# Layer 1's quantised FFN as a step pipeline in written order on four engines

## The chip, the cores and the metric

One NeuronCore of a Trainium2 chip runs the whole program. The metric is the device time of one execution in microseconds (us). The engines are called as the profile calls them: PE (TensorE, matrix products and transposes), DVE (VectorE), ACT (ScalarE), POOL (GpSimd) and SP (SyncE, which issues most transfers).

## The reference

A four-layer gated network on `x` of 128 x 64 x 128 floats. Each layer adds a gated cross-attention and a gated FFN of the layer-normed `x`; the four attentions and the four FFNs differ from each other. Only layer 1's FFN matters here. Its two linear maps quantise activations row by row to whole numbers of 8 bits and the weights to -1, 0 and 1:

```python
def rmsnorm(x):
    return x * jax.lax.rsqrt(jnp.mean(x * x, axis=-1, keepdims=True) + EPS)
def act_quant(x):
    scale = 127.0 / jnp.clip(jnp.max(jnp.abs(x), axis=-1, keepdims=True), 1e-05)
    q = jnp.clip(jnp.round(x * scale), -128.0, 127.0) / scale
    return x + jax.lax.stop_gradient(q - x)
def bitlinear(x, w, b):
    xq = act_quant(rmsnorm(x))
    wq = weight_quant(w)
    return jnp.einsum('bsd,fd->bsf', xq, wq) + b
...
    h = bitlinear(x, w1, b1)            # 128 -> 512
    h = jax.nn.gelu(h, approximate=False)
    return bitlinear(h, w2, b2)         # 512 -> 128
...
x = x + jnp.tanh(g_ffn[1]) * _L1_ffn_ref(_layernorm(x, axis=-1), ...)
```

## The kernel before

The 8192 tokens are 64 tiles of 128 rows (`NT` = 64). `x` stays in on-chip memory in float32 (`x_sb`) through all layers. The program is written in Python as a sequence of engine instructions; a scheduler then chooses each engine's order of instructions from its own estimates, within the data dependences, and sets the semaphores. Where a piece of code stands in a `tc.manual_schedule(engines=...)` block, the engines named follow the order in which the instructions are written. The scheduler may also pull instructions of a later stage into an earlier one.

Layer 1's FFN is `bit_ffn`. It runs over the 64 tiles in groups of `G` = 8:

- `bit_normal(g)` (L1472, POOL): eight `tensor_scalar` of 128x128, `xn_g` = the layer norm of the group's tiles, from the columns `nm` and `rstd`.
- `bit_sizes(g)` (L1484 to L1494, DVE): the rows' absolute maxima, one reduction of 128x1024, and a chain of small operations on 128x8 (`steps`, L1362 to L1369), which gives the factors `up` and `dn` and, in three bfloat16 pieces, the factor `inv` of the bias.
- `bit_whole(g, h)` (L1502, L1505, DVE): rounds four tiles of `xn_g` to whole numbers. It is called for the two halves.
- `first(g)` (L1535 to L1545): eight PE transposes of 128x128 (`pxq`), two copies by ACT (`xqT`), two transposes of the `inv` pieces (`pinv`) and a copy by ACT (`invT`).
- `second(k)`: two matmuls of 512 columns into `ph` (L1554 and L1556, PE), GELU into `h` (L1560, ACT), the square with its sum (`sq`, L1563, ACT), and the row maxima of `h` (`am`, L1564, DVE).
- `third`, once a group, when all eight tiles have their sum and maximum: 17 small DVE operations on 128x8, each of which needs the one before it (L1572, `quick_root` at L216 to L222, `steps`); its last result is `up` (L1369).
- `fourth(i)`: two `tensor_scalar` of 128x512 that round `h` in place (L1578, L1579; on POOL, and on DVE for every second tile of the last group, called `own`), four PE transposes (`phq`, L1582), ACT's copy to `hqT` (L1584), four matmuls into `py` (L1587, PE), and `residual`: `x_sb` += `dn` x `py` (L295, DVE) and the statistics `st` of the new `x` (L198, DVE). Every four tiles POOL first adds the gated bias `b2g` to `x_sb` (L1608).

The loop has steps i = 0 to `NT` + `LAG`, with `LAG` = `G` + 3 = 11: step i calls `second` for tile i and `fourth` for tile i - 11. `third` is called at the end of a group's last step. The next group's `bit_normal`, `bit_sizes` and the halves of `bit_whole` are called in steps k = 1, 3, 5 and 6 of a group. Four further pieces of DVE work are spread into the loop: `norms_of` with its root (L225 to L262; small operations on 128x32) for the second half of the tiles at i = 10, the root mean squares of that half (`rms_square`, L242) at i = 18, and the norms that the next attention needs at i = 56 and 64. None of this is in a `manual_schedule` block, so that the calls give the data dependences, and the scheduler the order.

The accumulators in PSUM are `pt`, `ph`, `pt4` and `py`, two buffers each. `hqT` has two buffers, `h` has `LAG` + 4 = 15, `xn_g` two.

Ahead of `bit_ffn` stands attention 1 (`head_attention(1, ...)`). Its lines in the prediction are the reciprocal L1004 and the transposes L1022 at the end of an attention step, which turn the heads' outputs; the next step's work on PE is queued behind them. Group 0's `bit_normal` is called within attention 1 by a plan; other early parts of the FFN get there by the scheduler's choice.

Of the kernel before, what the change touches and what calls it, by code (L numbers as in the profile page):

```python
# [14 lines left out]
ALU = mybir.AluOpType  # L15
AX = mybir.AxisListType
PE = mybir.EngineType.PE
SP = mybir.EngineType.SP
ACT = mybir.EngineType.Activation
DVE = mybir.EngineType.DVE  # L20
POOL = mybir.EngineType.Pool
# [5 lines left out]
P = 128  # L27
D = 128
# [13 lines left out]
class Net:  # L42
# [1315 lines left out]
    def steps(self, am, r, size, up, down, inverse=None):  # L1358


        nc = self.nc
        nc.vector.tensor_mul(am, am, r)  # L1362
        nc.vector.tensor_scalar_max(am, am, 1e-5)
        nc.vector.tensor_scalar(down, am, size, None, ALU.mult)
        nc.vector.reciprocal(am, am)
        if inverse is not None:
            nc.vector.tensor_scalar(inverse[0], am, inverse[1], None, ALU.mult)
        nc.vector.tensor_mul(am, am, r)
        nc.vector.tensor_scalar_mul(up, am, 127.0)  # L1369
# [141 lines left out]
    def bit_ffn(self):  # L1511

        nc, tc, NT = self.nc, self.tc, self.NT
        G = 8
        NG = NT // G


        LAG = G + 3  # L1520
        t1, t2, less, size2, r1 = self.t1, self.t2, self.less, self.size2, self.r1
        self.next_stats()
        with ExitStack() as st:
            work = st.enter_context(tc.tile_pool(name="bf", bufs=2))
            psum = st.enter_context(tc.tile_pool(name="bf_ps", bufs=2, space=PSUM))

            def first(g):

                b = self.bit_xn.pop(g)
                xn, dn = b["xn"], b["dn"]  # L1530
                xT = []
                for h in range(0, G, 4):
                    pt = psum.tile([P, 4, P], F32, tag="pt", name="pxq")
                    for k in range(4):
                        nc.tensor.transpose(pt[:, k, :], xn[:, h + k, :], self.ident)  # L1535
                    t = work.tile([P, 4, P], BF16, tag="xqT", name="xqT", bufs=4)
                    nc.scalar.activation(t, pt, AF.Identity, bias=less)
                    xT.append(t)
                pi = psum.tile([P, 2, P], BF16, tag="pt", name="pinv")
                for h in range(2):  # L1540
                    nc.tensor.transpose(
                        pi[:, h, :], self.inv[g % 2][:, h].rearrange("p k x -> p (k x)"), self.identb
                    )
                inv = work.tile([P, 2, P], BF16, tag="invT", name="invT")
                nc.scalar.copy(inv, pi)  # L1545
                hid = {}
                ss = work.tile([P, G], F32, tag="ss", name="ss")
                am = work.tile([P, G], F32, tag="am2", name="am2")
                return xT, inv, dn, hid, ss, am

            def second(k, xT, inv, dn, hid, ss, am):

                ph = psum.tile([P, FF], F32, tag="ph", name="ph")
                nc.tensor.matmul(ph, lhsT=xT[k // 4][:, k % 4, :], rhs=t1, start=True, stop=False)  # L1554
                rows = slice(32 * (k % 4), 32 * (k % 4) + 32)
                nc.tensor.matmul(  # L1556
                    ph, lhsT=inv[rows, k // 4, :], rhs=self.b1p[rows, :], start=False, stop=True
                )
                hid[k] = work.tile([P, FF], F32, tag="h", name="h", bufs=LAG + 4)
                gelu = nc.scalar.activation(hid[k], ph, AF.Gelu, scale=dn[:, k : k + 1])  # L1560
                self.last_own = gelu.ins.name
                sq = work.tile([P, FF], F32, tag="sq", name="sq")
                nc.scalar.activation(sq, hid[k], AF.Square, accum_out=ss[:, k : k + 1])  # L1563
                nc.vector.tensor_reduce(  # L1564
                    am[:, k : k + 1], hid[k], AX.X, ALU.max, apply_absolute_value=True
                )

            def third(ss, am):
                up = work.tile([P, G], F32, tag="up2", name="up2")
                dn = work.tile([P, G], F32, tag="dn2", name="dn2")  # L1570
                r = work.tile([P, G], F32, tag="r2", name="r2")
                nc.vector.tensor_scalar(ss, ss, 1.0 / FF, RMS_EPS, ALU.mult, ALU.add)  # L1572
                self.quick_root(r, ss, work, G)
                self.steps(am, r, size2, up, dn)
                return up, dn

            def fourth(i, k, h, up, dn, eng):
                eng.tensor_scalar(h, h, up[:, k : k + 1], MAGIC, ALU.mult, ALU.add)  # L1578
                eng.tensor_scalar(h, h, MAGIC + 127.0, MAGIC - 128.0, ALU.min, ALU.max)  # L1579
                pt = psum.tile([P, 4, P], F32, tag="pt4", name="phq")  # L1580
                for c in range(4):
                    nc.tensor.transpose(pt[:, c, :], h[:, c * P : (c + 1) * P], self.ident)  # L1582
                hT = work.tile([P, 4, P], BF16, tag="hqT", name="hqT")
                nc.scalar.activation(hT, pt, AF.Identity, bias=less)  # L1584
                py = psum.tile([P, D], F32, tag="py", name="py")
                for c in range(4):
                    nc.tensor.matmul(  # L1587
                        py, lhsT=hT[:, c, :], rhs=t2[:, c * D : (c + 1) * D],
                        start=(c == 0), stop=(c == 3),
                    )  # L1590
                self.residual(i, py, dn[:, k : k + 1])

            self.bit_sizes(0)
            self.bit_whole(0, 0)
            self.bit_whole(0, 4)
            groups, scales = {}, {}
            for i in range(NT + LAG):
                g, k = i // G, i % G
                if i < NT:
                    if k == 0:  # L1600
                        groups[g] = first(g)
                    second(k, *groups[g])
                if i >= LAG:
                    j = i - LAG
                    if j % 4 == 0:

                        x = self.x[:, j : j + 4, :]
                        nc.gpsimd.tensor_tensor(  # L1608
                            x, x, self.b2g.unsqueeze(1).to_broadcast([P, 4, D]), ALU.add
                        )  # L1610

                    own = j >= NT - G and j % 2
                    up, dn = scales[j // G]
                    fourth(j, j % G, groups[j // G][3][j % G], up, dn, nc.vector if own else nc.gpsimd)
                if i < NT and k == G - 1:
                    scales[g] = third(*groups[g][4:])
                if g + 1 < NG:
                    if k == 1:
                        self.bit_normal(g + 1)
                    elif k == 3:  # L1620
                        self.bit_sizes(g + 1)
                    elif k in (5, 6):
                        self.bit_whole(g + 1, 4 * k - 20)
                half = NT // 2
                if i == 10:
                    v = self.norms_of(half, half, self.st6_for, nc.vector)
                    self.norms_root(half, half, v)
                if i == 18:
                    ms = self.rms_square(half, half, v, nc.vector)
                    self.quick_root(r1[:, half:], ms, self.stat, half)  # L1630

                if i == NT - 8:
                    self.norm_columns()
                    v = self.norms_of(0, half, self.st6, nc.vector)
                    self.norms_root(0, half, v)
                if i == NT:
                    v = self.norms_of(half, NT // 4, self.st6, nc.vector)
                    self.norms_root(half, NT // 4, v)
        self.bit_stack.close()


# [564 lines left out]
```

## Time and profile before

| | |
|---|---|
| time, median of 3 runs (lowest to highest) | 2637.76 us (2636.06 to 2638.65) |
| the profiled execution: its time | 2637.47 us |
| its span, first to last instruction | 2635.7 us |
| mean granted TensorE clock | 0.911 of full speed |
| layer 1's FFN, first `pxq` transpose to the last `st` | about 1286 to 1475.5 us of the span |

The profile is of one execution. Its busy shares are means over stages that differ much; a stage is read by giving the views a window of time. In a line of the groups stand the line of the code, the engine, the operation, what it writes and reads, how many there were, the busy time in us and the mean of one in ns, and then the engine's idle time just before these instructions with what ended most of it. In a line of the timeline stand the start and the duration in us.

### The profile page before, as it was taken

The numbers are of one execution on the slowest core, as the hardware profiler recorded it, in microseconds if no ns is written. First come the engines' busy times: TensorE is split into PE (matmuls) and PEld (weight loads), VectorE is DVE, ScalarE is ACT, GpSimd is POOL, SyncE is SP. The second block draws the span as 40 slices with busy tenths as digits, with TensorE's granted clock in tenths as the row PEclk, the third lists the DMA queues.
The fourth block names the chain that finished last, engine by engine and source line by source line (L and its number), as shares of the span: only waits on it lengthen the run. The fifth ranks groups of instructions, "written<-read, shape, count | busy, mean of one in ns | idle before, by whom it ended". The sixth has DMA issues, their size and how long they took to land.

```text
span 2635.7 us, 75540 instructions
## 1 busy us (share of the span) xinstructions
PE 2200.8 (83%) x31658; PEld 1694.6 (64%) x31658; DVE 1548.2 (59%) x4442; ACT 1354.3 (51%) x2697; POOL 1053.9 (40%) x1309
## 2 busy tenths in 40 slices
PE   5999999999984978969767799998499867777597
PEld 4777777777773756757434576766499745555465
DVE  5544455454553337666677657676577588888432
ACT  3445454444442424546577455554377557777242
POOL 2122242233234552131266313634566662444444
PEclk9999999999996988989777899998699879888699
DMA  9997000000002141000000001111233541111121
GB/s 235 259 233 154 14 20 24 10 24 20 15 17 74 54 130 38 19 14 15 5 1 1 21 20 35 47 30 37 62 94 91 154 120 34 38 36 36 50 63 44
DMA packets 215364, 157.42 MB, mean 60 GB/s; under 512 B 27236, under 2 KB 191983, under 8 KB 215024
## 3 DMA queue, kind: packets, MB, share of 16 engines
q1 hardware_dynamic: 193744, 117.22, 18.4%
q0 software_dynamic: 16640, 32.22, 3.6%
q8 instruction: 250, 4.10, 0.7%
q10 hardware_dynamic: 4640, 3.15, 0.5%
q14 instruction: 90, 0.74, 0.1%
HBM read 68.62 MB, written 86.31 MB: 59 GB/s over the span
## 4 chain that ended last, share of the span: by engine, by line
PE 57%; DVE 18%; ACT 9%; POOL 5%; DMA 5%; issue 4%; SPq 0%; DVEq 0%; POOLq 0%; ACTq 0%
PE pqk L423 9%; PE ph L2009 5%; PE py L519 4%; PE pv L445 4%; PE po L505 3%; PE pav L982 3%; PE py L2030 2%; PE sb L924 2%; PE ph L1276 2%; PE sc L461 2%; PE pt L489 2%; PE pye L1295 2%; ACT low L965 2%; PE sb L931 2%; ACT low L963 2%
## 5 line engine op out<-in xcount | busy, mean ns | idle before, releaser
L478 POOL TENSOR_TENSOR a<-a,sm 128x1024 f32<-128x1024 f32 x64 | 121.7, 1901 | 449.3 <-DVE sm L477 228.6
L936 ACT ACTIVATE aT<-sb 128x512 f32<-128x512 f32 x256 | 132.1, 603 | 170.4 <-PE sb L931 170.4
L897 DVE TENSOR_REDUCE mpad<-sa 128x8 f32<-128x512 f32 x256 | 159.0, 684 | 85.6 <-PE sa L892 85.5
L524 DVE TENSOR_TENSOR x_sb<-x_sb,py 128x128 f32<-128x128 f32 x64 | 18.4, 288 | 284.2 <-PE py L519 284.2
L492 ACT COPY aT<-pt 128x512 f32<-128x512 f32 x128 | 68.8, 589 | 207.4 <-PE pt L489 207.4
L2040 POOL DMA_INDIRECT outs<-ye,to x136 | 133.7, 983 | 78.1 <-DVE ye L2036 54.4
L1875 POOL DMA_INDIRECT slots<-x_sb,fc_r x128 | 124.8, 975 | 96.8 <-DVE fc_r L1223 46.8
L786 POOL TENSOR_SCALAR xn<-x_sb,gn_nm,gn_r 128x128 f32<-128x128 f32 x128 | 57.7, 463 | 255.9 <-PE pxn L801 171.7
L982 PE MATMUL pav<-aT,vb 128*32 128x64 f32 x6144 | 127.0, 235 | 29.9 <-DVE aT L968 20.0
L423 PE MATMUL pqk<-xnT,L_Wq 128*128 128x256 f32 x512 | 120.9, 390 | 21.4 <-ACT xnT L415 21.4
L982 PEld LDWEIGHTS pav<-aT,vb 128*32 128x32 f32 x6144 | 106.0, 119 | 48.3 <-DVE aT L968 24.1
L2009 PE MATMUL ph<-xT,gw 128*128 128x128 f32 x1088 | 133.8, 277 | 0.0
L445 PE MATMUL pv<-L_Wv,ctxT 128*64 128x512 f32 x480 | 129.5, 618 | 0.0
L519 PEld LDWEIGHTS py<-L_wog,oT 128*128 128x128 f32 x1024 | 124.2, 192 | 7.4 <-DVE oT L510 4.2
L1295 PEld LDWEIGHTS pye<-L_w,hT 128*128 128x128 f32 x1024 | 119.1, 192 | 14.3 <-issue 11.2
L2009 PEld LDWEIGHTS ph<-xT,gw 128*128 128x128 f32 x1088 | 128.1, 194 | 0.2 <-issue 0.2
L519 PE MATMUL py<-L_wog,oT 128*128 128x128 f32 x1024 | 125.0, 275 | 3.8 <-DVE oT L510 3.8
L423 PEld LDWEIGHTS pqk<-xnT,L_Wq 128*128 128x128 f32 x512 | 96.0, 192 | 41.1 <-ACT xnT L415 29.1
L1295 PE MATMUL pye<-L_w,hT 128*128 128x128 f32 x1024 | 119.2, 275 | 0.0
L505 PEld LDWEIGHTS po<-aT,v 64*64 64x64 f32 x4096 | 77.7, 136 | 63.3 <-ACT aT L492 51.5
L1276 PE MATMUL ph<-xeT,L_w 128*128 128x512 f32 x256 | 117.4, 602 | 0.0
L963 ACT ACTIVATE low<-low 128x512 f32<-128x512 f32 x128 | 80.3, 628 | 70.6 <-DVE low L956 70.4
(363 smaller groups left out, 5932.3 us busy)
## 6 DMA issues: line engine op xcount, KB each, us to landing
slots<-zero SPq DMA_DIRECT2D x80, 528.0 KB
ctxT<-in_ctxT_dram SPq DMA_DIRECT2D x63, 256.0 KB
y<-outs SPq DMA_DIRECT2D x24, 512.0 KB
xe<-slots SPq DMA_DIRECT2D x136, 66.0 KB
xe<-slots SPq DMA_DIRECT2D x32, 264.0 KB
L_w<-in_L_ffn_W_dram SPq DMA_DIRECT2D x32, 256.0 KB
outs<-fxn SPq DMA_DIRECT2D x16, 256.0 KB
out_dram<-x_sb SPq DMA_DIRECT2D x16, 256.0 KB
```

The source lines that it names most:

```text
L423: nc.tensor.matmul(ps[:, cc, :], lhsT=wt[:, (c + cc) * P : (c + cc + 1) * P], rhs=rhs, start=True, stop=True,)
L445: nc.tensor.matmul(ps[h * S : (h + 1) * S], lhsT=tok, rhs=wv[:, h], start=True, stop=True)
L505: nc.tensor.matmul(po[h][x * S : (x + 1) * S, s, tok], lhsT=v[rows, b, 2 * s + x, :], rhs=aT[rows, 2 * s + x, tok], start=True, stop=True,)
L519: nc.tensor.matmul(py, lhsT=oT[:, h, s, :], rhs=w["wog"][:, h, s, :], start=h == 0 and s == 0, stop=h == 1 and s == 3,)
L897: nc.vector.reduce_max(mpad[:, j, 0:8], sc[j].rearrange("p b c k -> p (b c) k"), axis=AX.X)
L936: exp = nc.scalar.activation(aT[:, j], sc[j], AF.Exp)
L963: ln = self.nc.scalar.activation(low, low, AF.Ln, bias=1.0, scale=-1.0)
L982: nc.tensor.matmul(pav[32 * j : 32 * j + 32, b, t, :], lhsT=vb[:, 4 * (b0 + b) + j, t, :], rhs=aT[:, j, b, t, :], start=True, stop=True,)
L1276: nc.tensor.matmul(ph, lhsT=w["w1"][:, e, c * P : (c + 1) * P], rhs=x, start=True, stop=True)
L1295: nc.tensor.matmul(py[:, t, :], lhsT=h[:, c, t * P : (t + 1) * P], rhs=w["w2"][:, e, c, :], start=(c == 0), stop=(c == 3),)
L2009: nc.tensor.matmul(ph[:, 2 * t + c, :], lhsT=gw[j][:, t, c * P : (c + 1) * P], rhs=xT[j // 4][:, j % 4, :], start=True, stop=True,)
L2040: put = nc.gpsimd.indirect_dma_start(out=self.outs2, out_offset=bass.IndirectOffsetOnAxis(ap=to[q][:, j % 4 : j % 4 + 1], axis=0), in_=y[: ...
```

## The change

`second` loses its square and its maxima, which become `squares` (ACT) and `largest` (DVE). `fourth` is split into `whole` (the two roundings), `turn` (the four transposes and `hqT`) and `down` (the four matmuls and the residual). One step of the loop now issues, in this order: `largest` of the tile before; `third` of the group before, if the step begins a group; `second` of tile i; `whole` of tile i - 10, with `b2g` ahead of every fourth; `turn` of tile i - 11; `squares` of tile i; `down` of tile i - 12; and then the next group's preparation: `bit_normal` at k = 1, `bit_sizes` at k = 3, the halves of `bit_whole` at k = 4 and 5 (were 5 and 6), and `first` at k = 7 (was at the start of the next step). The last two pieces of norms move from i = 56 and 64 to 58 and 66. The whole loop stands in `tc.manual_schedule(engines={PE, ACT, DVE, POOL})`. Group 0's `bit_sizes` and `bit_whole` stay ahead of the block.

```diff
--- before.py
+++ after.py
@@ -1559,8 +1559,12 @@
                 hid[k] = work.tile([P, FF], F32, tag="h", name="h", bufs=LAG + 4)
                 gelu = nc.scalar.activation(hid[k], ph, AF.Gelu, scale=dn[:, k : k + 1])
                 self.last_own = gelu.ins.name
+
+            def squares(k, xT, inv, dn, hid, ss, am):
                 sq = work.tile([P, FF], F32, tag="sq", name="sq")
                 nc.scalar.activation(sq, hid[k], AF.Square, accum_out=ss[:, k : k + 1])
+
+            def largest(k, xT, inv, dn, hid, ss, am):
                 nc.vector.tensor_reduce(
                     am[:, k : k + 1], hid[k], AX.X, ALU.max, apply_absolute_value=True
                 )
@@ -1574,14 +1578,19 @@
                 self.steps(am, r, size2, up, dn)
                 return up, dn
 
-            def fourth(i, k, h, up, dn, eng):
+            def whole(k, h, up, eng):
                 eng.tensor_scalar(h, h, up[:, k : k + 1], MAGIC, ALU.mult, ALU.add)
                 eng.tensor_scalar(h, h, MAGIC + 127.0, MAGIC - 128.0, ALU.min, ALU.max)
+
+            def turn(h):
                 pt = psum.tile([P, 4, P], F32, tag="pt4", name="phq")
                 for c in range(4):
                     nc.tensor.transpose(pt[:, c, :], h[:, c * P : (c + 1) * P], self.ident)
                 hT = work.tile([P, 4, P], BF16, tag="hqT", name="hqT")
                 nc.scalar.activation(hT, pt, AF.Identity, bias=less)
+                return hT
+
+            def down(i, k, hT, dn):
                 py = psum.tile([P, D], F32, tag="py", name="py")
                 for c in range(4):
                     nc.tensor.matmul(
@@ -1593,49 +1602,69 @@
             self.bit_sizes(0)
             self.bit_whole(0, 0)
             self.bit_whole(0, 4)
-            groups, scales = {}, {}
-            for i in range(NT + LAG):
-                g, k = i // G, i % G
-                if i < NT:
-                    if k == 0:
-                        groups[g] = first(g)
-                    second(k, *groups[g])
-                if i >= LAG:
+            def steps():
+
+
+
+                groups, scales, hT = {0: first(0)}, {}, {}
+                for i in range(NT + LAG + 1):
+                    g, k = i // G, i % G
+                    if 0 < i <= NT:
+
+                        largest((i - 1) % G, *groups[(i - 1) // G])
+                        if k == 0:
+                            scales[g - 1] = third(*groups[g - 1][4:])
+                    if i < NT:
+                        second(k, *groups[g])
+                    j = i - LAG + 1
+                    if 0 <= j < NT:
+                        if j % 4 == 0:
+
+                            x = self.x[:, j : j + 4, :]
+                            nc.gpsimd.tensor_tensor(
+                                x, x, self.b2g.unsqueeze(1).to_broadcast([P, 4, D]), ALU.add
+                            )
+
+                        own = j >= NT - G and j % 2
+                        whole(
+                            j % G, groups[j // G][3][j % G], scales[j // G][0],
+                            nc.vector if own else nc.gpsimd,
+                        )
                     j = i - LAG
-                    if j % 4 == 0:
-
-                        x = self.x[:, j : j + 4, :]
-                        nc.gpsimd.tensor_tensor(
-                            x, x, self.b2g.unsqueeze(1).to_broadcast([P, 4, D]), ALU.add
-                        )
-
-                    own = j >= NT - G and j % 2
-                    up, dn = scales[j // G]
-                    fourth(j, j % G, groups[j // G][3][j % G], up, dn, nc.vector if own else nc.gpsimd)
-                if i < NT and k == G - 1:
-                    scales[g] = third(*groups[g][4:])
-                if g + 1 < NG:
-                    if k == 1:
-                        self.bit_normal(g + 1)
-                    elif k == 3:
-                        self.bit_sizes(g + 1)
-                    elif k in (5, 6):
-                        self.bit_whole(g + 1, 4 * k - 20)
-                half = NT // 2
-                if i == 10:
-                    v = self.norms_of(half, half, self.st6_for, nc.vector)
-                    self.norms_root(half, half, v)
-                if i == 18:
-                    ms = self.rms_square(half, half, v, nc.vector)
-                    self.quick_root(r1[:, half:], ms, self.stat, half)
-
-                if i == NT - 8:
-                    self.norm_columns()
-                    v = self.norms_of(0, half, self.st6, nc.vector)
-                    self.norms_root(0, half, v)
-                if i == NT:
-                    v = self.norms_of(half, NT // 4, self.st6, nc.vector)
-                    self.norms_root(half, NT // 4, v)
+                    if 0 <= j < NT:
+                        hT[j] = turn(groups[j // G][3][j % G])
+                    if i < NT:
+                        squares(k, *groups[g])
+                    j = i - LAG - 1
+                    if 0 <= j < NT:
+                        down(j, j % G, hT.pop(j), scales[j // G][1])
+                    if g + 1 < NG:
+                        if k == 1:
+                            self.bit_normal(g + 1)
+                        elif k == 3:
+                            self.bit_sizes(g + 1)
+                        elif k in (4, 5):
+                            self.bit_whole(g + 1, 4 * k - 16)
+                        elif k == 7:
+                            groups[g + 1] = first(g + 1)
+                    half = NT // 2
+                    if i == 10:
+                        v = self.norms_of(half, half, self.st6_for, nc.vector)
+                        self.norms_root(half, half, v)
+                    if i == 18:
+                        ms = self.rms_square(half, half, v, nc.vector)
+                        self.quick_root(r1[:, half:], ms, self.stat, half)
+
+                    if i == NT - 6:
+                        self.norm_columns()
+                        v = self.norms_of(0, half, self.st6, nc.vector)
+                        self.norms_root(0, half, v)
+                    if i == NT + 2:
+                        v = self.norms_of(half, NT // 4, self.st6, nc.vector)
+                        self.norms_root(half, NT // 4, v)
+
+            with tc.manual_schedule(engines={PE, ACT, DVE, POOL}):
+                steps()
         self.bit_stack.close()
 
 
```

## The prediction

> **What bounds the kernel now.** I read the page's head first. No engine fills the span, so the stage that changes has to be read by itself.
>
> ```profile
> span 2635.7 us, 75540 instructions
> PE 2200.8 (83%) x31658; PEld 1694.6 (64%) x31658; DVE 1548.2 (59%) x4442; ACT 1354.3 (51%) x2697; POOL 1053.9 (40%) x1309
> ```
>
> Layer 1's FFN runs from the first `pxq` transpose at 1286.15 us to the last `x_sb`/`st` at about 1475.5, 189 us; attention 2's first transfer follows at 1475.30. A table of windows gives, for the 23 us from 1383 to 1406, PE 15.8 us busy, DVE 17.2, ACT 15.9, POOL 16.7: again nobody is full. So I took the waits of that stretch (us in total, times, longest):
>
> ```profile
> ACT hqT L1584 <- PE phq L1582: 46.1, 23, 7.1
> POOL h L1578 <- DVE up L1369: 30.3, 5, 8.1
> PEld phq L1582 <- POOL h L1579: 27.7, 12, 5.5
> DVE x_sb L295 <- PE py L1587: 23.0, 21, 3.1
> DVE am L1484 <- POOL xn_g L1472: 17.8, 6, 3.4
> ```
>
> They form a ring. POOL waits for `up`, the last result of `third`; DVE does `third` in pieces behind L1484 of `bit_sizes`; L1484 waits for `bit_normal` on POOL, which stands behind the eight tiles' rounding that `up` released. POOL resumes with a new group at 1313.26, 1336.88, 1360.22, 1383.38, 1406.51, 1425.23, 1443.05 and 1462.47 us: periods of 23.1 to 23.6 while a later group is being prepared, 17.8 to 19.4 afterwards, and a tail of 13.1. The groups of instructions give the prices (busy us, mean ns):
>
> ```profile
> L1578 POOL TENSOR_SCALAR h<-h,up 128x512 f32<-128x512 f32 x60 | 43.9, 741 | 58.3 <-DVE up L1369 30.3 <-ACT h L1560 25.8
> L1564 DVE TENSOR_REDUCE am<-h 128x1 f32<-128x512 f32 x64 | 42.3, 675 | 1.7 <-ACT h L1560 1.7
> L295 DVE SCALAR_TENSOR_TENSOR x_sb<-py,dn,x_sb 128x128 f32<-128x128 f32 x64 | 22.2, 346 | 23.3 <-PE py L1587 23.0
> L198 DVE BATCH_NORM_STATS2 st<-x_sb 128x6 f32<-128x128 f32 x68 | 19.0, 285 | 0.7
> L1362 DVE TENSOR_TENSOR am<-am,r 128x8 f32<-128x8 f32 x14 | 2.9, 204 | 0.1
> ```
>
> DVE's timeline shows what a written order costs there. First a dependent chain by itself, then two chains interleaved (start, duration):
>
> ```profile
> 1460.58 0.17 DVE L222 SCALAR_TENSOR_TENSOR r<-qr_a,qr_y 128x8 f32<-128x8 f32 x1
> 1460.78 0.17 DVE L1362 TENSOR_TENSOR am<-am,r 128x8 f32<-128x8 f32 x1
> 1460.98 0.17 DVE L1363 TENSOR_SCALAR am<-am 128x8 f32<-128x8 f32 x1
> ```
> ```profile
> 1307.46 0.17 DVE L1368 TENSOR_TENSOR am<-am,r 128x8 f32<-128x8 f32 x1
> 1307.54 0.18 DVE L1490 CAST inv<-inv 128x24 bf16<-128x24 f32 x1
> 1307.62 0.17 DVE L216 TENSOR_SCALAR qr_y<-ss 128x8 int32<-128x8 int32 x1
> ```
>
> A small op costs 0.20 us behind the op that it needs, 0.08 behind another. Last, an older place, inside attention 1, where the scheduler has put this FFN's first groups:
>
> ```profile
> 1162.92 4.92 POOL L1608 TENSOR_TENSOR x_sb<-x_sb,b2g 128x512 f32<-128x512 f32 x4
> ```
> ```profile
> 1164.12 3.82 DVE L1362 TENSOR_TENSOR am<-am,r 128x8 f32<-128x8 f32 x2
> 1169.19 0.35 DVE L1004 RECIPROCAL r<-po 128x32 f32<-128x32 f32 x1
> ```
> ```profile
> 1170.23 0.66 PE L1022 MATMUL pot<-ident,o 128*128 128x128 f32 x2 [17.96 <-DVE inv L1490]
> ```
>
> DVE's L1362 stood behind POOL ops with no gap between them, and PE sat idle for 17.96 us because L1004 was queued behind this FFN's chain.
>
> **The change, part by part.** Work added: none. By the built programs' instruction orders, SP's queue is the same, and so is every instruction's size; only the order on PE, ACT, DVE and POOL differs, in this stage and, for what is pulled ahead, in attention 1.
>
> Removed: the ring. `bit_normal(g+1)` now stands on POOL ahead of the rounding that needs `third(g-1)`, so L1484's 17.8 us of waiting go; `turn` comes one step behind `whole` and `down` one behind `turn`, so most of the phq, hqT and py waits go. What is late next is the fullest engine. Per group of eight: ACT (pitches from its timeline: GELU 0.57, hqT 0.57, square with its accumulator read 0.61) 8 x 1.75 + 1.45 for `first` = 15.5 us; POOL 8 x 1.48 + 3.45 (`bit_normal`) + 2 x 1.26 (b2g) = 17.8; PE as measured, 15.8. DVE is fullest, since its chains now stand whole in the written order:
> - `largest` 0.59, L295 to the dependent L198 0.39, L198 0.21: 1.19 a tile, 9.5 a group.
> - `third`: 17 dependent ops at 0.20 = 3.4.
> - `bit_sizes`: L1484 1.2 and about 11 ops at 0.20 = 3.4. `bit_whole`: twice 4 x 0.20 + 0.42 = 2.5.
> Together 18.8 us without contention, say 19.0.
>
> Contention: `bit_sizes` at k = 3 and the first half of `bit_whole` at k = 4 fall into POOL's train of rounding, which `third` starts at k = 0 and which lasts 14.4 us. Where L1362 and L1363 met such a train, they took 0.36 and 0.49 us. For 12 ops that is 12 x 0.17 = 2.0 in `bit_sizes`, 0.75 in `bit_whole` (four L1502 took 1.57 for 0.8), 0.3 in `third`: a period of 22.0. Low end 0 (19.0, no collision), high end 0.72 an op, the pitch of POOL's ops (12 x 0.52 = 6.2, period 26). I take the middle, because it is measured for these ops and this train.
>
> The Trainium skill, page "SBUF — State Buffer", section "Who interferes with whom", says that a DVE op with two SBUF inputs or in a two-port mode shares a port pair with GpSimd as an exclusive lock, so that whoever issues second blocks for the whole instruction. It speaks against this change: with every op held for one POOL op the six prepared periods would last 26 us and the sum would be about 2667. The trace shows the block (3.82 us above) but also two ops passing per POOL op in a train with gaps.
>
> The norms also move. `norms_of` with its root is 18 ops on 32 columns at 0.225, 3.9 us, and with contention 6.4; the rms part is 14 ops, 2.9, contended 5.0. The sum against the resumes above:
> - Ramp: `third(0)` no longer shares DVE with the rms chain and `bit_sizes`; it follows the eighth GELU. 1306.9 instead of 1313.26: -6.3 (between -3 and -7).
> - Two periods with norms: 22 + 6.4 less 3.4 for residuals that have not begun = 25.0, against 23.6; 22 + 5.0 less 1.6 = 25.4, against 23.3: together +3.5.
> - Four of 22.0 against 23.2, 23.1, 18.7 and 17.8 = 82.8: +5.2. Before had prepared two groups ahead; the last two of its periods have no `bit_sizes` in them.
> - One without preparation, with norms: 9.5 + 3.4 + 6.4 = 19.3 against 19.4: 0.
> - Tail: after the last `third` DVE has 18 ops of norms (3.7), its own four roundings (4 x 0.9 = 3.6), eight tiles of L295/L198 and the last tile's run through POOL, PE, ACT and DVE in turn, about 19.5 against 13.1: +6.4 (between +2 and +9).
> The stage: +8.8 us.
>
> Attention 1: group 1's `bit_sizes` and the four b2g adds are no longer pulled ahead. L1004 starts at about 1164.3 instead of 1169.19: -4.9 (0, if another wait takes the stall's place, to -8). Nothing covers this stall, as PE waits at the end of a chain.
>
> Net +3.9 on the profiled execution, 2637.47 us (span 2635.7 and 1.8 around it; the median of three is 2637.76): **2641.5 us**. This case's own range, from the ramp, tail and attention bounds, is 2635 to 2649.
>
> The Trainium skill's page "VectorE: DVE Perf Modes", section "The DRAIN you can't avoid", measures eight chained copies at 13.88 us with and without semaphores between them, so order and waits would cost nothing. The trace differs: 0.08 against 0.20. By the page the chains would lose about 3.4 us a period, and the sum would be near 2617.
>
> **The rivals.**
> - **Collisions are rare: faster.** The mean of L1362 in the stage is 204 ns over 14, hardly over its free 0.17, so POOL's train may seldom touch the chains. My contention is 6 x 3.0 in the periods and about 11 in norms and tail, 29 in all; with a third of it the time is 2641.5 - 19 = 2622.5, with none 2612.5. Against it: in before, those ops mostly ran while POOL waited for `up`, which `bit_sizes` now does not. It decides if fewer than one op in three is held.
> - **Bursts stop PE: slower.** The PSUM tiles ph, pt4 and py are two deep, and DVE stays away from py for 3.4 to 6.6 us at `third` and `bit_sizes`. PE in written order then waits in `down`, with the next step's ph and transposes queued behind it, and ACT starves. DVE catches up on two tiles in 2.4 us; PE's step is 1.75 to 2.0 us at full clock, 2.4 to 2.8 at the 0.72 granted here, and a GELU (0.57) follows. If that refill exceeds 2.4 us DVE idles after each burst, 1 to 1.5 us, two bursts in seven groups: about +17.5, 2659 us. For it: PE waited for `x_sb` 6.5 us in all already in before. Against: DVE, not PE, is the fullest, and a backlog absorbs part.
> - **The order hardly matters.** A new ring of the same length forms through `third`: 2637.5. The trace names no such ring.
>
> **How the numbers follow.** This kernel's measurement can tell about 0.2%, 5.3 us, from no change: 2632.5 to 2643. The forecast's case has 0.42, of which 0.18 lies in that band and 0.24 above; rare collisions 0.33, all faster; bursts 0.21, all slower; no effect 0.04. So faster 0.33, same 0.22, slower 0.45. The range runs through both rivals, from 2614 (between a third and none of the contention) to 2662 (bursts and a little more).
>
> **What would show it.** In the changed profile: no L1484 wait and `third` unbroken, 3.4 us long (ring and chains right); resumes of POOL 22 us apart (19 or less: collisions rare; 24 and over: bursts, with PE py waiting for `x_sb`); L1362 and L1363 of `bit_sizes` near 0.36 us; a tail near 19.5; the idle before L1022 near 13. If PE or ACT has no idle time left in the stage, the bound is misnamed.

## The result, and the profile after

The changed kernel takes 2653.09 us (median of 4 runs, 2650.27 to 2655.45) against 2636.91 us (4 runs, 2635.95 to 2638.65): ratio 1.0056, 95% interval 1.0044 to 1.0068. It is slower by 16 us; 2641.5 had been forecast, with a range of 2614 to 2662. The profiled execution took 2652.91 us, 15.4 more than the one before. The head of its page:

```profile
span 2651.2 us, 75546 instructions
PE 2209.6 (83%) x31658; PEld 1700.0 (64%) x31658; DVE 1585.0 (60%) x4442; ACT 1359.9 (51%) x2697; POOL 1054.1 (40%) x1309
```

DVE alone has clearly more busy time (1585.0 against 1548.2 us), for the same 4442 instructions. The waits of the stage (1280 to 1500 us; us in total, times, longest):

```profile
POOL h L1582 <- DVE up L1369: 49.7, 7, 9.7
PE py L1596 <- DVE x_sb L295: 42.7, 12, 7.7
ACT h L1560 <- PE ph L1556: 34.9, 18, 7.4
DVE x_sb L295 <- PE py L1596: 7.2, 10, 1.2
```

The others wait for DVE: POOL for `up`, PE for the residual that empties `py`, ACT for PE behind it. DVE itself waits for 7.2 us, and L1484 no longer appears at all: the ring is gone. The windows of two periods (length; busy and count of PE, PEld, DVE, ACT, POOL; granted clock; DMA share; GB/s):

```profile
1376.10:1398.90 22.80, 17.09 (x93) 10.19 (x91) 21.53 (x65) 16.37 (x36) 16.87 (x26) 0.72 0.00 1
1422.40:1446.50 24.10, 18.93 (x93) 11.44 (x91) 21.17 (x65) 16.92 (x36) 13.06 (x18) 0.64 0.00 1
```

The groups (busy us, mean ns, idle before) and pieces of DVE's timeline show why. The roundings, reductions and residuals cost no more than they did, but L1364 has a mean of 471 ns:

```profile
L1582 POOL TENSOR_SCALAR h<-h,up 128x512 f32<-128x512 f32 x60 | 42.0, 700 | 68.3 <-DVE up L1369 49.7 <-ACT h L1560 14.6
L1568 DVE TENSOR_REDUCE am<-h 128x1 f32<-128x512 f32 x64 | 42.8, 672 | 5.2 <-ACT h L1560 5.2
L295 DVE SCALAR_TENSOR_TENSOR x_sb<-py,dn,x_sb 128x128 f32<-128x128 f32 x64 | 21.9, 342 | 7.2 <-PE py L1596 7.2
L1364 DVE TENSOR_SCALAR dn<-am,t_size 128x8 f32<-128x8 f32 x15 | 7.1, 471 | 0.5
```

In the kernel before, the same line had a mean of 240 ns:

```profile
L1364 DVE TENSOR_SCALAR dn<-am,t_size 128x8 f32<-128x8 f32 x14 | 3.4, 240 | 0.0
```

`third`, while POOL waits, runs at 0.20 us an operation (3.40 us in all). `bit_sizes`, in the middle of POOL's rounding, does not:

```profile
1397.10 0.17 DVE L221 SCALAR_TENSOR_TENSOR qr_a<-qr_a,ss 128x8 f32<-128x8 f32 x1
1397.30 0.17 DVE L222 SCALAR_TENSOR_TENSOR r<-qr_a,qr_y 128x8 f32<-128x8 f32 x1
...
1381.21 0.17 DVE L1362 TENSOR_TENSOR am<-am,r 128x8 f32<-128x8 f32 x1
1381.41 0.58 DVE L1363 TENSOR_SCALAR am<-am 128x8 f32<-128x8 f32 x1
1382.03 1.32 DVE L1364 TENSOR_SCALAR dn<-am,t_size 128x8 f32<-128x8 f32 x1
1383.38 0.20 DVE L1365 RECIPROCAL am<-am 128x8 f32<-128x8 f32 x1
```

The 1.32 us cover a b2g add of 1.27 us, which POOL started at 1382.04. The norms at i = 58 fare worse:

```profile
1451.26 0.57 DVE L232 TENSOR_TENSOR no_a<-no_a 128x32 f32<-128x32 f32 x1
1451.87 0.18 DVE L233 TENSOR_SCALAR no_a<-no_a 128x32 f32<-128x32 f32 x1
1451.96 0.63 DVE L234 TENSOR_TENSOR no_v<-st 128x32 f32<-128x32 f32 x1
1452.62 1.30 DVE L235 TENSOR_TENSOR no_v<-no_v,no_a 128x32 f32<-128x32 f32 x1
1453.95 0.62 DVE L236 TENSOR_SCALAR no_v<-no_v 128x32 f32<-128x32 f32 x1
```

And in attention 1 the stall has become shorter:

```profile
1164.11 0.66 PE L1022 MATMUL pot<-ident,o 128*128 128x128 f32 x2 [13.04 <-DVE o L1015]
```

To compare kernels, the stage is taken below from POOL's first `bit_normal` in it to POOL's first operation of attention 2, by the timeline. "Periods" are the times between POOL's resumes with a new group.

| kernel | ratio to before (95%) | stage from | to | length | ramp; periods; tail |
|---|---|---|---|---|---|
| before | 1 | 1288.23 | 1475.38 | 187.2 | 25.0; 23.6 23.3 23.2 23.1 18.7 17.8 19.4; 12.9 |
| the change | 1.0056 (1.0044 to 1.0068) | 1280.19 | 1490.95 | 210.8 | 19.3; 26.2 27.6 22.8 22.8 23.5 24.2 23.5; 20.9 |
| e1, third and bit_sizes braided | 0.9991 (0.9977 to 1.0005) | 1311.73 | 1504.15 | 192.4 | 20.4; 23.5 23.7 21.4 21.2 21.4 18.7 22.0; 20.2 |
| e2, norms braided too | 0.9952 (0.9934 to 0.9971) | 1312.35 | 1491.70 | 179.4 | 21.3; 21.7 21.4 21.3 21.4 21.4 19.1 17.2; 14.7 |
| e3, POOL rounds 64 columns | 0.9977 (0.9966 to 0.9988) | 1310.94 | 1499.55 | 188.6 | 19.3; 23.7 24.7 20.1 22.0 20.1 20.0 20.5; 18.3 |
| e4, DVE left free | 0.9998 (0.9988 to 1.0008) | 1316.28 | 1505.94 | 189.7 | 20.3; 23.4 23.9 23.9 23.9 24.7 18.6 19.3; 11.8 |
| e5, all engines free | 1.0006 (0.9995 to 1.0017) | 1289.29 | 1478.79 | 189.5 | 25.0; 23.4 23.9 23.6 24.0 19.4 18.8 18.8; 12.7 |
| e6, before's calls in written order | 1.0316 (1.0298 to 1.0333) | 1282.47 | 1554.95 | 272.5 | 20.0; 27.5 30.8 32.3 31.6 31.8 32.6 32.7; 33.2 |
| e7, eight py tiles | 1.0085 (1.0063 to 1.0106) | 1283.39 | 1491.30 | 207.9 | 19.3; 26.2 27.7 22.5 22.9 22.6 22.4 22.9; 21.5 |
| e8, before, nothing of group 1 ahead | 0.9997 (0.9984 to 1.0010) | 1282.36 | 1474.95 | 192.6 | 24.6; 22.9 23.4 23.3 23.3 19.4 19.2 23.0; 13.5 |
| e9, e2 with POOL's train rearranged | 0.9933 (0.9912 to 0.9954) | 1280.56 | 1455.81 | 175.3 | 23.0; 20.1 20.0 19.6 21.1 18.6 18.8 17.4; 16.7 |
| e10, e9 with DVE's own roundings at once | 0.9936 (0.9920 to 0.9953) | 1280.68 | 1457.83 | 177.2 | 23.3; 20.1 20.0 20.0 19.4 20.8 20.0 17.1; 16.5 |
| e11, only the norms braided | 0.9990 (0.9980 to 0.9999) | 1280.05 | 1469.45 | 189.4 | 19.7; 21.9 22.6 23.5 23.5 23.5 22.8 17.2; 14.7 |
| e12, shorter root in third | 1.0044 (1.0027 to 1.0060) | 1282.06 | 1487.09 | 205.0 | 18.1; 24.9 26.9 24.2 22.3 22.3 23.0 22.6; 20.9 |

e1 to e4 ran in a session in which the kernel before, too, took longer, 2845.86 us. Their traces have the additional time outside the stage (in e1 the stage starts at 1311.73 us instead of 1280.19, and 1339 us follow it instead of 1160). So ratios are to the kernel before of the same session, and the lengths of the stage are compared across; its groups on DVE and ACT have the same means in e1 as in the change (L1568 672 ns and L1560 686 in both, L295 343 and 342).

For the change, the stage starts 8.0 us earlier and lasts 23.6 us longer: together 15.6, where the profiled executions differ by 15.4.

### The profile page after: what moved, and what is told of

Read it like the earlier page. It is cut to its first block, busy times and chain, and to the rows that moved or that the text cites. A ratio compares the mean times of both kernels' runs of the same rounds, so it can differ in the third digit from the quotient of the medians.

```text
span 2651.2 us, 75546 instructions
## 1 busy us (share of the span) xinstructions
PE 2209.6 (83%) x31658; PEld 1700.0 (64%) x31658; DVE 1585.0 (60%) x4442; ACT 1359.9 (51%) x2697; POOL 1054.1 (40%) x1309
## 5 line engine op out<-in xcount | busy, mean ns | idle before, releaser
L897 DVE TENSOR_REDUCE mpad<-sa 128x8 f32<-128x512 f32 x256 | 158.8, 682 | 85.4 <-PE sa L892 85.3
L524 DVE TENSOR_TENSOR x_sb<-x_sb,py 128x128 f32<-128x128 f32 x64 | 18.4, 288 | 284.2 <-PE py L519 284.2
L423 PE MATMUL pqk<-xnT,L_Wq 128*128 128x256 f32 x512 | 120.6, 389 | 21.4 <-ACT xnT L415 21.4
L423 PEld LDWEIGHTS pqk<-xnT,L_Wq 128*128 128x128 f32 x512 | 95.8, 192 | 41.0 <-ACT xnT L415 29.1
```

The lines of the kernel that those rows point to most:

```text
L423: nc.tensor.matmul(ps[:, cc, :], lhsT=wt[:, (c + cc) * P : (c + cc + 1) * P], rhs=rhs, start=True, stop=True,)
L897: nc.vector.reduce_max(mpad[:, j, 0:8], sc[j].rearrange("p b c k -> p (b c) k"), axis=AX.X)
```

## The experiments

**Order or calls?** e5 takes the `manual_schedule` block away and keeps all the new calls and places; e4 leaves only DVE out of it; e6 puts before's own loop into such a block.

```diff
-            with tc.manual_schedule(engines={PE, ACT, DVE, POOL}):
-                steps()
+            steps()                                                  # e5
+            with tc.manual_schedule(engines={PE, ACT, POOL}):        # e4
+                steps()
```

> The changed kernel's calls (split parts, moved first, moved norms) with no engine held to the written order: the scheduler decides on all four. It separates the splitting of the calls from the order. Theory: the loss lies in DVE's written order, so without it the time falls to about that of the version in which only DVE was left free, ratio to before 0.995 to 1.003. Rival: the new places of the calls cost by themselves; then the ratio stays at 1.004 or above.

> The changed kernel with DVE left to the scheduler; PE, ACT and POOL follow the written order. Theory (DVE's written order is the cause): the scheduler interleaves the chains with the reductions and residuals as it did before, 0.08 instead of 0.20 us an operation, and the ring of before is gone, so 2615 to 2635, below before. Rival (the pipeline of calls itself, or PE in written order, costs the time): 2645 to 2660. A third possibility is that the scheduler pulls group 1's chain back into attention 1, which gives the stall of 17.96 us before L1022 back: +5 on either.

> The kernel before with its own calls, undivided, put into the written order on PE, ACT, DVE and POOL: the order alone, without the pipeline. Theory: in one step PE does ph, phq and then waits in py for hqT, which ACT does behind GELU and square of the same step, so a step is the chain ph 0.9 + GELU 0.7 + square 0.6 + hqT 0.6 + py 0.45, about 3.3 us, 26 and more a group with first and the chains of DVE: the stage is 60 to 100 us longer than the 187 of before, ratio 1.023 to 1.038. Rival (the order by itself is what costs, not the chains on DVE, and the pipeline gains nothing): the same as the changed kernel, 1.006.

Measured: 1.0006, 0.9998 and 1.0316. With DVE free, the stage is within 2.5 us of before's 187.2, with the order on the other three engines (189.7) and without it (189.5). So what the change loses, it loses through DVE's written order; the new calls and PE's, ACT's and POOL's order cost little. But e4 did not gain what was expected of it, because the ring came back with the scheduler's DVE order. In e4's timeline L1484 stands ahead of `third` again and waits for `bit_normal`:

```profile
1400.95 1.22 DVE L1484 TENSOR_REDUCE am<-xn_g 128x8 f32<-128x1024 f32 x1 [5.30 <-POOL xn_g L1472]
```

Its prepared periods are mostly 23.9 us, where the change has 22.8 in its best two. Against the kernel before, the change wins only in its ramp (5.7 us) and in its third and fourth period (22.8 against 23.2 and 23.1); it loses in the first two, the last three and the tail. e6 shows that the order by itself, with undivided calls, costs 85 us of stage.

**The collisions.** e3 makes POOL's operations short, and so leaves columns 64 to 511 of `h` unrounded:

```diff
             def whole(k, h, up, eng):
+                h = h if eng is nc.vector else h[:, 0:64]
```

> The changed kernel with POOL's two roundings of a tile done on 64 of the 512 columns only (the other columns of h stay unrounded), so that POOL's train of about 14 us becomes one of some 5 us and mostly lies before bit_sizes. DVE's order and chains are untouched. Theory of collisions: bit_sizes falls from 4.8 to 6.2 us to 3.4, bit_whole from 3.9 to 2.5, the norms pieces by 2 to 4 us each: periods of 22.8 become about 20, in all -20 to -30 us, 2623 to 2633. If only the exposed chains count and collisions are small: within 8 us of 2653. If PE's pace is the bound: the same as now.

Measured: 0.9977, and a stage 22.2 us shorter than that of the change, with DVE's order untouched. The trace shows where: from POOL's first resume on, DVE's chains (`third`, `bit_sizes`, `bit_whole` and the norms, each from its first operation to the next reduction or residual) take 88.8 us together, against 108.2 in the change, and DVE's waits 6.0 against 8.6. So 19.4 of the 22.2 us are DVE's own operations, which POOL's rounding had held up, and not a shorter way through POOL; `third`, which runs while POOL waits, kept its 3.4 us. `bit_normal` and b2g are still there and still hold DVE. In e3 the norms at i = 58 run at 0.22 us an operation, except where a b2g add stands:

```profile
1467.31 0.19 DVE L220 TENSOR_TENSOR qr_a<-qr_y 128x32 f32<-128x32 f32 x1
1467.54 0.19 DVE L221 SCALAR_TENSOR_TENSOR qr_a<-qr_a,no_v 128x32 f32<-128x32 f32 x1
...
1468.24 1.15 DVE L221 SCALAR_TENSOR_TENSOR qr_a<-qr_a,no_v 128x32 f32<-128x32 f32 x1
```

**The norms and the sizes.** To braid means here: the calls of two chains are recorded and then issued in turn, one operation of each. e11 braids the norms into `third`, e1 `bit_sizes`, e2 both.

```diff
                         if k == 0:
-                            scales[g - 1] = third(*groups[g - 1][4:])
+                            scales[g - 1], a = recorded(lambda vec: third(vec, *groups[g - 1][4:]))
+                            more = []
+                            if g + 1 < NG:                                   # e1, e2
+                                more.append(recorded(lambda vec: self.bit_sizes(g + 1))[1])
+                            if i in norms:       # e2, e11: i = 8, 16, 56, 64
+                                more.append(recorded(norms[i])[1])
+                            braid(a, *more)
...
+                            if g + 2 < NG:                                   # e1, e2, at k == 7
+                                self.bit_normal(g + 2)
```

> The changed kernel with only the four pieces of norms moved: braided into third at i = 8, 16, 56 and 64, while POOL waits, bit_sizes left at k = 3. Theory: they took 7.9 + 6.0 + 8.5 + 6.7 = 29 us of DVE by themselves, in collision with POOL; braided they add about 1.6 to 2.5 each, so the stage is 15 to 20 us shorter, ratio 0.998 to 1.000. If the norms were not on the path: 1.005.

> The changed kernel (2653.1 us) with one thing moved: from the second group on, bit_sizes is issued together with third at the start of a group, one operation of each chain in turn, instead of alone at k = 3; bit_normal is issued two steps earlier for that. Theory (DVE's unbroken dependent chains, and their meeting POOL's rounding, set the period): third and bit_sizes took 3.4 + 4.8 to 6.2 us one after the other; braided they should take 1.2 + 28 x 0.10 = about 4.0 while POOL waits for up. That saves 4 to 5 us in six periods, 24 to 30 in all, less what PE then takes at its own pace (18.9 us busy in a period): periods 19 to 20 instead of 22.8 to 24.1, time 2627 to 2635. Rival (PE is stopped by bursts on DVE and its own pace sets the period): the burst is as long or longer, so the time stays within 5 us of 2653.

> As the kernel with third and bit_sizes braided, and the four pieces of norms braided into third as well (at i = 8, 16, 56 and 64 instead of 10, 18, 58 and 66). In the changed kernel these took 7.9, 6.0, 8.5 and 6.7 us by themselves, in the middle of POOL's rounding; free of it 3.9, 2.9, 3.9 and 3.6. Theory: braided, while POOL waits, each adds about 18 x 0.09 = 1.6 us instead, so 5 to 6 us less in four places, 20 us in all where DVE is the bound, less where PE is: time 2610 to 2622. Rival: no gain over the first braid beyond 5 us.

Measured: 0.9990, 0.9991 and 0.9952. e11 alone takes back 21.4 us of stage, all in the four periods or tails that held norms (26.2 to 21.9, 27.6 to 22.6, 23.5 to 17.2, 20.9 to 14.7); the others did not get shorter by more than 1.4. This is not only what POOL had added to the norms: braided, they cost hardly anything, half a us more than `third` alone. The braid at i = 56, `third` with 18 operations of norms, takes 3.94 us for 35 operations, 0.11 each:

```profile
1433.94 0.22 DVE L2186 TENSOR_TENSOR no_a<-st 128x32 f32<-128x32 f32 x1
1434.07 0.16 DVE L2186 TENSOR_TENSOR qr_a<-qr_y 128x8 f32<-128x8 f32 x1
1434.19 0.19 DVE L2186 TENSOR_TENSOR no_a<-no_a 128x32 f32<-128x32 f32 x1
1434.30 0.16 DVE L2186 SCALAR_TENSOR_TENSOR qr_a<-qr_a,ss 128x8 f32<-128x8 f32 x1
```

e1 gave less than expected of it: the stage fell by 18.4 us instead of 24 to 30, and its prepared periods stop at about 21.3 instead of 19 to 20, where POOL waits for `up` for only 2.8 us. e2 takes off a further 13, not 20. POOL's train is the next limit.

**POOL's train.** e9 is e2 with `bit_normal` put last in the train and b2g into the middle of a half group.

```diff
-                            if g + 2 < NG:
-                                self.bit_normal(g + 2)
+                        if k == 1 and g + 2 < NG:
+                            self.bit_normal(g + 2)
...
-                        if j % 4 == 0:
-                            x = self.x[:, j : j + 4, :]
+                        if j == 0 or j % 4 == 2 and j + 2 < NT:
+                            first_x = j and j + 2
+                            x = self.x[:, first_x : first_x + 4, :]
```

> The kernel with third, bit_sizes and the norms braided, and POOL's train rearranged: bit_normal(g+2) is called at k = 1 of group g, so that it stands last in the train and runs while DVE does the braided chains, and b2g is called in the middle of a half group instead of at its start, so that no 1.27-us operation stands before up. In the braided kernel a prepared period was 21.3 us = POOL's train of 17.1 busy and a DVE braid of about 4 that followed it. Theory: bit_normal's 0.44-us operations hold DVE little, so the period becomes 14.4 + about 4.3 = 18.7 us, six times 2.5 us less: ratio to before about 0.990. Rival (the braid is held as much by bit_normal, or PE at 16 us busy sets the pace): 0.995, as without the rearrangement.

Measured: 0.9933, and 2624.29 us against 2639.84: the fastest of these kernels together with e10, and between what was expected (0.990) and its rival (0.995). The period is 20.0, not 18.7: the train took 14.8 us and the braid 5.0 beside `bit_normal`, whose operations hold DVE after all, if little. In e9's timeline of POOL, the end of the train, the eight `bit_normal` operations, and the resume:

```profile
1337.75 0.61 POOL L1583 TENSOR_SCALAR h<-h 128x512 f32<-128x512 f32 x1
1338.46 3.44 POOL L1472 TENSOR_SCALAR xn_g<-x_sb,nm,rstd 128x128 f32<-128x128 f32 x8
1343.67 0.69 POOL L1582 TENSOR_SCALAR h<-h,up 128x512 f32<-128x512 f32 x1 [1.77 <-DVE up L2190]
```

**The tail.** e10 is e9 with the four own roundings issued at once behind the last `third` (and left out of their later steps).

```diff
                             braid(a, *more)
+                            if i == NT:
+                                for m in range(1, G, 2):
+                                    whole(m, groups[g - 1][3][m], scales[g - 1][0], nc.vector)
```

> The braided kernel with the rearranged train, and DVE's four own roundings of the last group issued at once behind third instead of one every second step. There the last 16.7 us ran in steps of 3.2 us for two tiles, because each own rounding stood behind the residual of an earlier tile. Theory: the tail falls to 11 to 13 us, ratio 0.990 to 0.992 where that kernel had 0.9933. Rival (POOL's four roundings and two b2g adds, 8.5 us, and the run through PE, ACT and DVE behind them set the tail): no change.

Measured: no change (0.9936; tail 16.5 against 16.7). It was a miss. Part of the reason is again POOL: next to POOL's roundings and b2g add of the same tile size, the eight operations took 6.6 us instead of 3.6. These 3.0 us lie on the chain that ended last; behind them it runs for about 9 us through PE, ACT and the residuals. The tail missed what was expected by 3.5 to 5.5 us; the rest is not explained.

```profile
1442.45 0.82 DVE L1582 TENSOR_SCALAR h<-h,up 128x512 f32<-128x512 f32 x1
1443.30 1.37 DVE L1583 TENSOR_SCALAR h<-h 128x512 f32<-128x512 f32 x1
```

**Is it PE, stopped by bursts?** e7 lets PE run up to eight tiles ahead of the residual; e12 shortens DVE's chain itself (its factor is less exact).

```diff
+                if i % 4 == 0:                                       # e7
+                    py4[0] = psum.tile([P, 4, D], F32, tag="py", name="py")
-                py = psum.tile([P, D], F32, tag="py", name="py")
+                py = py4[0][:, i % 4, :]
...
-                self.quick_root(r, ss, work, G)
+                self.quick_root(r, ss, work, G, 1)                   # e12: 1 step of 3
```

> The changed kernel with four py tiles to a PSUM bank, so that eight instead of two can be outstanding while DVE is in a chain; PE then needn't stop in down. Theory (DVE is busy or in a dependent chain for all but 7 to 9 us of the stage, so PE's 42.7 us of waiting for x_sb cost little): -3 to -8 us against the changed kernel, ratio to before 1.002 to 1.005. Rival (bursts stop PE, and PE's pace sets the period): -15 us or more, ratio 1.000 or below.

> The changed kernel with one step of the root instead of three in third (the factor r is then less exact): 6 of its 17 dependent operations are gone, 1.2 us a group. Theory (DVE is the bound and every op of its chains counts in full): the stage is 8 x 1.2 = 9.6 us shorter, 7 to 10, ratio 1.002. Rival (PE's pace sets the period): less than 3 us, 1.005 to 1.006.

Measured: 1.0085 and 1.0044. e7's stage is 2.9 us shorter, where the rival wanted 15: PE's waits for the residual (42.7 us in the change, 53.7 in e7) were waits of an engine with time to spare. Its whole time is 10 us longer, though, and not in the stage: from the stage's end to the end of the program it took 1169.7 us against 1160.3 in the change, in code that is the same. Why is not settled; e12 and e6 have as much there (1169.3 and 1169.9). e12's stage is 5.7 us shorter of the 9.6 that were taken out (7 to 10 had been expected), and DVE's waits for `py` rose from 7.2 to 11.6 us, which is about the rest. So DVE is the bound, with PE close behind it. By time alone e12 (1.0044) can't be told from the change (1.0056).

**Attention 1 alone.** e8 is the kernel before with an ordering that keeps group 1's `bit_sizes` and the b2g adds out of attention 1.

```diff
+                        ops = self.bit_normal(g + 1)
+                        if g == 0:
+                            tc.add_manual_dep(ops[0].ins, self.last_own, ORDER, reason='not ahead of the stage')
...
+                    if j % 4 == 0:
+                        tc.add_manual_dep(add.ins, self.last_own, ORDER, reason='not ahead of the stage')
```

> The kernel before, with the last operation of bit_normal for... group 1 and the b2g adds held behind the stage's own GELUs by an ordering, so that the scheduler no longer puts group 1's bit_sizes and four b2g adds into attention 1. Only the part in attention 1 of the change. Theory: the idle time before L1022 falls from 17.96 to about 13 us, the stage starts 5 to 8 us earlier, and some of it is given back as group 1's preparation comes into the ramp (up to 4 us): ratio 0.997 to 0.9995. Rival: all of it is given back in the ramp, ratio 1.000 or above.

```profile
1166.52 0.66 PE L1022 MATMUL pot<-ident,o 128*128 128x128 f32 x2 [12.92 <-DVE o L1015]
```

The stall shrinks as predicted, from 17.96 to 12.92 us. Attention 1, from its first L897 to the stage, falls from 296.4 to 289.1 us, but the stage becomes 5.4 us longer: 0.9997, no change. What is given back lies not in the ramp but in the last periods (19.4 becomes 23.0). The preparations are not later there: in both kernels the last L1484 stands in the fourth period. But seven b2g adds of about 1.25 us now run in POOL behind the start of the fifth period (1399.90 us), where the kernel before has none. Whether they are the cause was not tested.

## Why the prediction was right in direction and short in size

The 2653.1 us lie outside the range of the forecast's own case (2635 to 2649). They lie inside the stated range because it runs through the rivals as well, which was luck for the forecast's sum. Its error in the stage (14.8 us) was larger than the one that is seen in the time (11.4 in the profiled execution), since the stage also starts 3.1 us earlier than forecast. The waits that the prediction shows are those of the whole stage, not of the 23 us named ahead of them.

- **The ring goes, DVE is the bound, its chains stand unbroken:** shown. No L1484 wait; `third` 3.40 us; 1.17 to 1.18 us a tile against 1.19 in the sum; from POOL's first resume on DVE waits 8.5 us (7.2 for `py`, 1.3 for ACT at L588, an early operation of the next attention); before, 23.0 for `py` and 17.8 at L1484.
- **Attention 1:** predicted -4.9; the idle time before L1022 fell by 4.92, and attention 1 by 6.1 (296.4 to 290.3). A further 1.9 us of the earlier start lies ahead of attention 1, where nothing differs.
- **Ramp:** predicted -6.3, measured -5.7.
- **Four plain periods:** predicted 22.0 each, measured 22.8, 22.8, 23.5 and 24.2: +5.3. `bit_sizes` took 4.8 to 6.2 us in collision (5.4 in the sum), `bit_whole` 3.0 to 3.9 (3.25); 3.1 us is DVE's waiting for `py` in the last two, where PE's clock was granted at 0.65 and 0.64 and its steps lasted 2.4 us while DVE waited. The sum had no such wait.
- **The norms: this term was mis-sized.** Contended they were put at 6.4, 5.0 and 6.4, and in the tail at a free 3.7, 21.5 us together. They took 7.9 (1300.31 to 1308.25), 6.0, 8.5 and 6.7, 29.1 together: 0.43 to 0.47 us an operation in the periods, not the 0.36 of the sum, because b2g adds stood in the train too; and the tail's piece met POOL's last roundings, which the sum overlooked. That is 7.6 of the 14.8 us by which the stage was underestimated (+23.6 against +8.8). e11, which moves nothing but the norms, makes the program as fast as before (0.9990); but it takes away their forecast cost, too, so it does not measure the error by itself.
- **The period without preparation:** predicted 19.3, measured 23.5: 2.1 from the norms, and 1.8 are waits of DVE (0.5 for `py`, 1.3 at L588).
- **Tail:** predicted 19.5, measured 20.9; its other parts were cheaper than estimated.
- **Rivals.** Rare collisions: refuted, e3 gains 22 us. Bursts that stop PE: its 2659 lies nearer to the result than the forecast does, and its sign, PE waiting for `x_sb`, came (42.7 us, against 6.5 before). But the sign does not tell the two apart. The rival's cost was DVE idle for want of `py`, about 17.5 us, and DVE's waits for `py` are 7.2 in the whole stage, 3.6 of them in the tail; e7 does not take more than 2.9 us off. Its PE step was also too long: 1.34 us where PE's rows are shortest (1377.50 to 1378.84), and 2.4 where they are longest, not 1.75 to 2.0 and up to 2.8. No effect: a ring through `third` did not form, as DVE's waits show.
- **The port rule of the Trainium skill** ("SBUF — State Buffer", "Who interferes with whom"). Its direction was right: the lengthened operations of the change have two inputs in SBUF or are a tensor_scalar or a cast (L1490, up to 0.49 us), while the reductions (672 ns, 675 before) and L295, with an input in PSUM, kept their durations. The price that the prediction worked out from it, one POOL operation for each DVE operation, was too high here: in POOL's train about every second small operation still took 0.17 to 0.19 us.
- **"The DRAIN you can't avoid" of the Trainium skill's page "VectorE: DVE Perf Modes".** Its 13.88 us with and without semaphores are for eight copies; that order would cost nothing was the prediction's reading of it. These runs differ from the reading: 0.20 us an operation in an unbroken chain, 0.11 in a braid of two.

## What to carry to other kernels

A written order removed the scheduler's bad placements here (L1484 ahead of `third`), but it also took away the interleaving by which the scheduler had small dependent operations start 0.08 us after another instead of 0.20; before fixing the order of an engine, list its chains and issue two or three of them in turn. Place DVE's small chains where POOL is waiting anyway: here four pieces of norms cost 29 us in POOL's train, and moving them alone to where POOL waits took 21 us off the stage (e11). When the busiest engine is freed, look at once for the next ring: in e9 it was POOL's train plus the braid, 14.8 + 5.0 us of a period of 20.0.

## What was not expected of the hardware

- DVE operations on 128x512 in SBUF collide with POOL's of the same size in both directions: in e10 seven of DVE's eight took 0.7 to 1.4 us instead of 0.43 to 0.48 (the longest beside a b2g add), and POOL's first stretched to 0.89 from 0.69.
- Next to `bit_normal`'s 0.44-us operations several of DVE's small ones took 0.20 to 0.27 us instead of about 0.16 (e9): a braid took 5.0 us there.
- The rest of the program, unchanged, took from 1160 (before, the change) to 1176 us (e9's profiled execution, the slowest of its four) behind the stage, e1 to e4 left aside; so differences under 10 us are better read from the stage than from the total.
